# Maxima on ScalarE's queue, normalisation a stage ahead with a second image buffer, staggered last steps

## The chip, the cores and the metric

The kernel runs on one core of one Trainium2 chip. The metric is the device time of one execution in microseconds, the median over the runs shown. All numbers here come from one profiled execution and three timed ones of the kernel before the change.

## What is computed

Sixteen images of 256 channels and 28 x 28 pixels go through a group normalisation, two "codebook" 3 x 3 convolutions with batch normalisation, a squeeze-and-excite gate and two residual additions, all in float32:

```python
def amm_conv3x3(x, centroids, w_sub, stride=1):        # C = 256 channels, k = 16 codes, s = 9 taps
    patches = conv_general_dilated_patches(x, (3, 3), (stride, stride), 'SAME')
    p = patches.reshape(B, C, s, Ho * Wo).transpose(0, 3, 1, 2)
    d = sum(p * p)[..., None] - 2.0 * einsum('bncs,cks->bnck', p, centroids) + sum(centroids * centroids)
    attn = softmax(-d, axis=-1)
    lut = einsum('cks,cso->cko', centroids, w_sub)
    return einsum('bnck,cko->bno', attn, lut)          # reshaped to B, 256, 28, 28

g = _gn(x)                                             # 32 groups
out = relu(bn(amm_conv3x3(g, centroids1, wsub1)))
out = bn(amm_conv3x3(out, centroids2, wsub2))
out = se_layer(out)                                    # mean, two small matmuls, sigmoid gate
return x + relu(out + g)
```

## The kernel before

One *stage* is one convolution of one image. The stages run in the order (0,0), (0,1), (1,0), (0,2), (1,1), (0,3), ...: the first convolution of image b+1 stands between the two convolutions of image b, so that the patches of one stage are prepared while another computes. After the first two stages and up to the last two, stages of the second and of the first convolution alternate; one of each is called a *period* here, and there are fourteen of them before the last pair.

A stage has 16 *units*: two pixel ranges (`PXT`: 384 and 400 of the 784 pixels) by eight groups of 32 channels. A unit runs through these steps:

- `patches`: SP (SyncE's queue) issues four loads of some 110 KB, the unit's rows, from the DRAM buffer `pat` into one of four `pt` tiles.
- `b_logits`, line 543: 16 small matmuls on PE; `b_exp`, line 601: two exponentials on ACT; `b_num`, line 611: 16 small matmuls; `b_turn`, lines 623 and 629: two transposes and a reciprocal on DVE; `c_scale`, line 639: products on POOL; `c_turn`, line 657: a transpose on DVE; `c_look`, line 675: the large 128 x 128 matmuls ("look-ups") that accumulate the output. A look-up is one matmul of the program and two in the trace.
- Four of the 16 units of a second-convolution stage are *maxed* (`MAXED`): their softmax needs a maximum first. Such a unit has its patches in a `pm` tile, and runs ahead: `a_logits` and `a_turn`, `a_max`, `m_turn` (line 575, the tile `mt`), then `m_out` (line 582) sends the maxima to DRAM (`dm`) and `m_in` (line 588) loads them back, spread, into rows of the `pm` tile, which `b_logits` then reads.

The order is written out by hand. `Plan` puts each step into a numbered slot, one slot for each unit, and into a position within the slot: `LOGITS, EXP, LOOK_A, NUM, TURN, SMALL, LOOK_B, MAX, LOOK_C, TURN_BACK, REST`. `emit` walks through slots and positions and issues the steps; every engine and every queue then works through its own instructions in that order. Within a unit's slot s the patches are issued at s - 3 (`lead`), and a maxed unit's first part starts at s - 5 (`lb`). Look-ups are spread over the slots, four or five in each, and two more in a slot that has a `MAX` step.

Around the units, each stage needs:

- `norm`: `load_x` (POOL's queue) brings an image into `xt` (784 KB), `gn_stats` on DVE, `gn_mean` and `gn_var` (small matmuls, small POOL operations), `gn_apply` on ACT writes the padded image `im0`.
- `prep`: `shift` (ACT copies `im` into two shifted `side` images) and twelve `to_pat` steps (line 454), each a 588 KB write from ACT's queue into a `pat` buffer in DRAM. There are three `pat` buffers, and in most of the run each convolution has one.
- `close`, after a second-convolution stage: `se_hidden`, `se_gate`, `se_scale`, then for four pieces of the image `gate` (ACT), and `finish`, which is a DVE operation (line 511), a ReLU on ACT (line 512) and an addition on POOL (line 513), and `store` on POOL's queue. `load_x` is called a second time for this residual. `xpool` has one buffer.

SP's and ACT's transfers share eight completion semaphores, which the program hands out in turn: a transfer is issued only when the one that had its semaphore before it, the eighth before it in the planned order, has landed, whichever of the two queues that one is on.

Within a period the slots are numbered 0 to 15 for the second-convolution stage and 16 to 31 for the first-convolution stage. The places before: `prep` of the next second convolution in slots 16 to 21 (two `to_pat` a slot), the residual's `load_x` in slot 16, `close` in 19 to 24, `norm`'s `load_x` in 25 and its steps in 28 to 32, `prep` of the next first convolution in slots 1 to 12 (one a slot).

Of the kernel before, what the change touches and what calls it, by code (L numbers as in the profile page):

```python
# [8 lines left out]
F32 = mybir.dt.float32  # L9
# [6 lines left out]
P = 128  # L16
H = W = 28
HW = H * W
# [51 lines left out]
def kernel(  # L70
# [71 lines left out]
    xpool = ctx.enter_context(tc.tile_pool(name="xpool", bufs=1))  # L142
# [97 lines left out]
    def scratch(n):  # L240
        return epool.tile([P, 2, 400], F32, tag="e", name="scratch").rearrange("p i m -> p (i m)")[:, :n]

    def sort_channels():
# [19 lines left out]
        row = scratch(C)  # L263
# [124 lines left out]
    epool = ctx.enter_context(tc.tile_pool(name="epool", bufs=4))  # L388
# [118 lines left out]
    def finish(b, k, i):  # L507

        y, xt = ys[b][0][half(k, i)], xs[b][half(k, i)]
        rstd, _ = nrm[b]  # L510
        nc.vector.scalar_tensor_tensor(y, xt, rstd[:, k : k + 1], y, op0=ALU.mult, op1=ALU.add)  # L511
        nc.scalar.activation(y, y, AF.Relu)  # L512
        nc.gpsimd.tensor_add(y, y, xt)
# [64 lines left out]
    def m_out(u):  # L578

        d = drot.tile([4 * 256, 32], F32, tag="dm", name="dm")  # L580
        for p0, n in ((0, P), (P, 96)):
            nc.sync.dma_start(view(d, 32 * p0, [[32, n], [256 * 32, 4], [1, 32]]), u["mt"][:n])
# [125 lines left out]
    class Plan:  # L708
# [12 lines left out]
        def emit(self):  # L721
            for n0, of in self.tiles:

                slots = [n0 + (LC + q) * self.step for q in range(NQ)]
                more = [2 if (s, MAX) in self.jobs else 0 for s in slots]
                k, room = 0, len(LOOKS) - sum(more)
                for q, s in enumerate(slots):
                    n = (q + 1) * room // NQ - q * room // NQ + more[q]
                    for i, (m, o, h) in enumerate(LOOKS[k : k + n]):
                        self.at(s, LOOK_A if i < 2 else LOOK_B if i < n - more[q] else LOOK_C, c_look, of[m], o, h)  # L730
                    k += n
            for key in sorted(self.jobs):
                for f, a in self.jobs[key]:
                    f(*a)

        def stage(self, l, b, pat, s0, maxed):
            at = self.at
            for pi, px in enumerate(PXT):
                n0 = s0 + pi * NQ * self.step
                of = []  # L740
                for m in range(NQ):
# [3 lines left out]
                    if m in maxed:  # L745
                        a = s - self.lb
                        at(a - self.lead, REST, patches, u)
# [5 lines left out]
                        at(a + 2, TURN_BACK, m_out, u)  # L753
                        at(a + 3, EXP, m_in, u)
# [25 lines left out]
        def close(self, b, ob, te):  # L780
# [36 lines left out]
    plan = Plan(1, 3, 5)  # L817
    for si, (l, b) in enumerate(stages):
        t = si * NS
        plan.stage(l, b, pat_of(l, b), t, () if l == 0 else MAXED)  # L820
        if l == 0 and b >= 1:
            t0 = t - NS - (1 if b == 1 else 4)
            plan.at(t0 - 3, REST, load_x, b, x[b])
            plan.norm(b, t0)
            plan.prep(0, pat_of(0, b), t0 + 5, 2 if b == 1 else 1)
        if l == 1:
# [3 lines left out]
            plan.close(b, out[b], t + NS + LC)  # L830
# [5 lines left out]
    for j in range(NCH):  # L836
        for s in range(9):
            plan.at(6 + s // 2, REST, place_wd2, j, s)
        for i in range(4):
            for t in range(4):  # L840
                plan.at(12 + i, REST, place_cw2, i, t, j)
            for t in range(2):
                plan.at(16 + i, REST, place_ws2, i, t, j)
            plan.at(20 + i, REST, place_tail, i, j)
    plan.at(16, REST, setup_codes, 1)
# [15 lines left out]
    with tc.If(flag > 0):  # L861
        with tc.For_i(0, B) as bi:
            load_x("g", x[bass.ds(bi, 1)].rearrange("o c n -> (o c) n"))
            plan = Plan(8, 2, 5)
            plan.norm("g", 0)
            plan.prep(0, d_pat[0], 5, 1)
            s0 = 28
            plan.stage(0, "g", d_pat[0], s0, range(NQ))
            plan.prep(1, d_pat[1], s0 + plan.end, 1)
            s1 = s0 + plan.end + 24  # L870
            plan.stage(1, "g", d_pat[1], s1, range(NQ))
            plan.at(s1 + plan.end - 4, REST, load_x, "g", x[bass.ds(bi, 1)].rearrange("o c n -> (o c) n"))
            plan.close("g", out[bass.ds(bi, 1)].rearrange("o c n -> (o c) n"), s1 + plan.end)
# [75 lines left out]
```

## Time and profile before

| what | value |
|---|---|
| median of 3 runs | 3377.37 us (3372.45 to 3379.37) |
| the profiled execution | 3372.49 us, span 3371.0 us |
| PE busy | 3042.2 us, 90% of the span |
| DVE, POOL, ACT busy | 2250.0, 1501.8, 1094.9 us |
| mean granted TensorE clock | 0.950 |
| DMA moved | 530.24 MB, 157 GB/s in the mean |

PE is the engine to read first: its idle time, and the stretches in which its clock is below one, are what stands above the work itself. Waits are listed with what ended them. Queues are named by the engine that issues on them, with a q (SPq, ACTq).

### The profile page before, as it was taken

Reading aid. Unit: us, or ns where it says so; the run is one execution under the profiler, and the core shown is the slowest. Engines: PE = TensorE matmul, PEld = TensorE weight load, DVE = VectorE, ACT = ScalarE, POOL = GpSimd, SP = SyncE. Lnnn points to the kernel's source line nnn. Section 1 sums busy time; section 2 is a strip of 40 time slices with the busy share of each in tenths; the row PEclk is TensorE's granted clock in tenths of the full one; section 3 lists DMA queues with packets and bytes.
Section 4 is the critical chain, followed back from the end, with each engine's and each line's share of the span. In section 5 each row is a group of like instructions: output and inputs, shape, how many; then the busy total and the mean of one; then the engine's idle time right before and its main releaser. Section 6 shows DMA issues by size and latency. Waiting matters only on the chain.

```text
span 3371.0 us, 94072 instructions
## 1 busy us (share of the span) xinstructions
PE 3042.2 (90%) x39838; PEld 1195.0 (35%) x39838; DVE 2250.0 (67%) x2756; ACT 1094.9 (32%) x1611; POOL 1501.8 (45%) x2165
## 2 busy tenths in 40 slices
PE   4878989999899999999999899999999899999997
PEld 2333333333333333333333333333333333333333
DVE  2355668676675767767676676767767576776785
ACT  2322333333333333333333333333333333333233
POOL 1333454454444445454454445445444444545444
PEclk9888999999999999999999999999999999999998
DMA  6755665746567565665746566475665747566542
GB/s 196 200 117 128 161 194 133 189 121 165 168 149 192 126 177 143 166 194 123 195 123 163 168 166 195 121 181 134 168 183 141 197 124 182 145 156 190 147 100 66
DMA packets 331902, 530.24 MB, mean 157 GB/s; under 512 B 93664, under 2 KB 251088, under 8 KB 331472
## 3 DMA queue, kind: packets, MB, share of 16 engines
q1 hardware_dynamic: 242512, 251.70, 29.8%
q10 hardware_dynamic: 82048, 233.89, 26.7%
q0 software_dynamic: 6912, 38.54, 3.4%
q8 instruction: 316, 5.18, 0.6%
q14 instruction: 114, 0.93, 0.1%
HBM read 269.96 MB, written 254.05 MB: 155 GB/s over the span
## 4 chain that ended last, share of the span: by engine, by line
PE 62%; DMA 16%; DVE 12%; issue 4%; ACT 2%; POOL 2%; SPq 1%; ACTq 1%; DVEq 0%; POOLq 0%
PE acc L675 35%; PE pair L611 13%; PE pair L543 12%; DMA pt<-pat 6%; DVE nt L623 4%; DMA pm<-dm 3%; DMA dm<-mt 3%; DMA pat<-side 2%; DVE q L657 2%; DMA pat<-im 2%; DVE y L511 2%; DVE rc L629 1%; DVE mx L567 1%; ACT e L601 1%; POOL k L639 1%
## 5 line engine op out<-in xcount | busy, mean ns | idle before, releaser
L675 PE MATMUL acc<-q,ws 128*128 128x384 f32 (+1 forms) x4096 | 1701.7, 537 | 0.0
L623 DVE STREAM_TRANSPOSE nt<-pair 128x832 f32<-128x832 f32 (+1 forms) x1024 | 978.3, 993 | 1042.8 <-PE pair L611 907.8
L639 POOL TENSOR_TENSOR k<-nt,rc 128x832 f32<-128x832 f32 (+1 forms) x512 | 803.5, 1569 | 1829.7 <-DVE rc L629 1827.4
L601 ACT ACTIVATE e<-pair 128x800 f32<-128x800 f32 (+1 forms) x1024 | 787.0, 820 | 1692.4 <-PE pair L543 1691.9
L675 PEld LDWEIGHTS acc<-q,ws 128*128 128x128 f32 x4096 | 721.8, 196 | 957.6 <-issue 641.2
L611 PE MATMUL pair<-e,cw 32*32 32x384 f32 (+1 forms) x16384 | 624.0, 527 | 83.6 <-ACT e L601 83.6
L543 PE MATMUL pair<-pt,wd 19*32 19x384 f32 (+1 forms) x14336 | 479.0, 513 | 76.2 <-DMA pt<-pat 75.7
L657 DVE STREAM_TRANSPOSE q<-k 128x832 f32<-128x832 f32 (+1 forms) x512 | 488.9, 955 | 0.8 <-POOL k L639 0.8
L629 DVE RECIPROCAL rc<-nt 128x104 f32<-128x104 f32 (+1 forms) x512 | 398.4, 778 | 17.6
L611 PEld LDWEIGHTS pair<-e,cw 32*32 32x32 f32 x16384 | 179.6, 106 | 452.5 <-ACT e L601 384.3
L543 PEld LDWEIGHTS pair<-pt,wd 19*32 19x32 f32 x14336 | 113.8, 104 | 364.3 <-issue 221.4
L645 POOL TENSOR_TENSOR tail<-nt,rc 128x104 f32<-128x104 f32 (+1 forms) x512 | 236.0, 461 | 0.0
L675 PE MATMUL acc<-qt,ws 128*128 128x400 f32 (+1 forms) x512 | 220.9, 514 | 0.0
L651 POOL TENSOR_TENSOR total<-total,nt 128x96 f32<-128x96 f32 (+1 forms) x448 | 208.9, 466 | 0.0
L543 PE MATMUL pair<-pm,wd 19*32 19x384 f32 (+3 forms) x4096 | 131.1, 541 | 77.4 <-DMA pm<-dm 71.0
L651 POOL TENSOR_TENSOR total<-total,rc 128x96 f32<-128x96 f32 (+1 forms) x448 | 177.2, 396 | 0.0
L562 DVE STREAM_TRANSPOSE z<-pair 128x768 f32<-128x768 f32 (+1 forms) x128 | 121.2, 985 | 12.8 <-PE pair L543 12.4
L675 PEld LDWEIGHTS acc<-qt,ws 128*128 128x128 f32 x512 | 93.4, 192 | 96.0 <-issue 43.9
L567 DVE TENSOR_REDUCE mx<-z 128x48 f32<-128x768 f32 (+1 forms) x128 | 120.8, 944 | 0.0
L512 ACT ACTIVATE y<-y 128x392 f32<-128x392 f32 x64 | 33.9, 529 | 176.4 <-DVE y L511 176.2
L543 PEld LDWEIGHTS pair<-pm,wd 19*32 19x32 f32 (+1 forms) x4096 | 31.1, 105 | 150.4 <-DMA pm<-dm 56.5
L664 DVE STREAM_TRANSPOSE qt<-tail 128x416 f32<-128x416 f32 (+1 forms) x128 | 69.9, 546 | 0.0
(105 smaller groups left out, 726.2 us busy)
## 6 DMA issues: line engine op xcount, KB each, us to landing
pat<-side ACTq DMA_DIRECT2D x256, 588.0 KB
pt<-pat SPq DMA_DIRECT2D x896, 112.5 KB
pt<-pat SPq DMA_DIRECT2D x896, 108.0 KB
pat<-im ACTq DMA_DIRECT2D x128, 588.0 KB
xt<-in_x POOLq DMA_DIRECT2D x32, 784.0 KB, 7.8
pm<-pat SPq DMA_DIRECT2D x128, 112.5 KB
pm<-pat SPq DMA_DIRECT2D x128, 108.0 KB
out_dram<-y POOLq DMA_DIRECT2D x16, 784.0 KB, 5.4
```

The costliest lines, as they stand in the source:

```text
L543: nc.tensor.matmul(ps[t // 2][c : c + 32, t % 2, :n], lhsT=wd[l][32 * i : 32 * i + rows, 4 * u["m"] + t, :], rhs=u["pt"][32 * i : 32 * i + ...
L562: nc.vector.transpose(z[:, : 64 * nb].rearrange("p (t m) -> p t m", t=2), ps[:, :, : 32 * nb])
L567: nc.vector.tensor_reduce(u["mx"][:, 2 * v : 2 * v + 2].rearrange("p t (j b) -> p t b j", j=2)[:, :, :nb], u["z"].pop(0)[:, : 64 * nb].rea ...
L601: nc.scalar.activation(e[:, :, :n], ps[:, :, :n], AF.Exp, scale=2.0)
L611: nc.tensor.matmul(u["nm"][t // 2][32 * i : 32 * i + 32, t % 2, :n], lhsT=cw[l][c : c + 32, 4 * u["m"] + t, :], rhs=es[t // 2][c : c + 32, ...
L623: nc.vector.transpose(nt[:, :nb, 2 * v : 2 * v + 2].rearrange("p b t r -> p t b r"), ps[:, :, : 32 * nb].rearrange("p t (b r) -> p t b r", ...
L629: nc.vector.reciprocal(rc[:, : 8 * nb], u["nt"][:, :, SUM])
L639: nc.gpsimd.tensor_tensor(q[:, :nb].rearrange("p b (a s) -> p (b a) s", s=8), nt[:, :, :8], rc.unsqueeze(2).to_broadcast([P, 8 * nb, 8]), ...
L645: nc.gpsimd.tensor_tensor(tails[key][:, :nb, 8 * (m % 4) : 8 * (m % 4) + 8], nt[:, :, 8].rearrange("p (b a) -> p b a", a=8), rc.rearrange( ...
L651: nc.gpsimd.tensor_add(t[:, : 8 * nb], t[:, : 8 * nb], v)
L657: nc.vector.transpose(q[:, :, : 32 * nb].rearrange("p h (b r) -> p h b r", r=32), u.pop("k")[:, :nb].rearrange("p b (h r) -> p h b r", h=2),)
L675: nc.tensor.matmul(accs[key][:, :n], lhsT=ws[l][:, 2 * m + h if h < 2 else 2 * NQ + m // 4, o * P : (o + 1) * P], rhs=u["q"][h][:, :n], st ...
```

## The change

1. `m_out` and `m_in` move from SP's queue to ACT's; the first part of a maxed unit starts six slots ahead and no longer five, its patches stay in the same slot; `m_out` goes from the end of slot s - 3 to its `TURN` position, `m_in` from `EXP` to `TURN` of slot s - 2.
2. `norm` and `prep` of the first convolution move a stage ahead. `xpool` gets two buffers (`epool` goes from four to two to make room, and the setup's scratch tiles move to other pools), `load_x` moves to slot 16, the same slot as the residual's, the statistics to 19 and 21, mean and variance to 23 and 24, `gn_apply` to 25 and 26, the twelve `to_pat` to slots 28 to 39, that is 28 to 31 and 0 to 7 of the next period. There are four `pat` buffers, two for each convolution.
3. `finish` is split into `finish`, `relu` and `residual`, one slot apart, with one piece of the image a slot (two a slot for the last two images); `store` moves from slot 24 to 27.
4. The look-ups between logits and numerators are half of a slot's, where they were always two: three in a slot of five.
5. The setup's 74 moves of rearranged weights go out four a slot in slots 6 to 24; they had been bunched by kind, up to eight a slot. `setup_codes(1)` moves from slot 16 to slot 20, the second image's `norm` two slots ahead.

```diff
-    d_pat = [dram.tile([NRT * ROWS, HW], F32, name=f"pat{i}") for i in range(3)]
+    d_pat = [dram.tile([NRT * ROWS, HW], F32, name=f"pat{i}") for i in range(4)]
-    xpool = ctx.enter_context(tc.tile_pool(name="xpool", bufs=1))
+    xpool = ctx.enter_context(tc.tile_pool(name="xpool", bufs=2))
-    epool = ctx.enter_context(tc.tile_pool(name="epool", bufs=4))
+    epool = ctx.enter_context(tc.tile_pool(name="epool", bufs=2))
...
         nc.vector.scalar_tensor_tensor(y, xt, rstd[:, k : k + 1], y, op0=ALU.mult, op1=ALU.add)
+
+    def relu(b, k, i):
+        y = ys[b][0][half(k, i)]
         nc.scalar.activation(y, y, AF.Relu)
-        nc.gpsimd.tensor_add(y, y, xt)
+
+    def residual(b, k, i):
+        y = ys[b][0][half(k, i)]
+        nc.gpsimd.tensor_add(y, y, xs[b][half(k, i)])
...
-            nc.sync.dma_start(view(d, 32 * p0, [[32, n], [256 * 32, 4], [1, 32]]), u["mt"][:n])
+            nc.scalar.dma_start(view(d, 32 * p0, [[32, n], [256 * 32, 4], [1, 32]]), u["mt"][:n])
-            nc.sync.dma_start(
+            nc.scalar.dma_start(
                 u["pt"][MROW + j :: 32, :, :n],
...
-                        self.at(s, LOOK_A if i < 2 else LOOK_B if i < n - more[q] else LOOK_C, c_look, of[m], o, h)
+                        self.at(s, LOOK_A if i < n // 2 + n % 2 - more[q] // 2 else LOOK_B if i < n - more[q] else LOOK_C, c_look, of[m], o, h)
...
                         a = s - self.lb
-                        at(a - self.lead, REST, patches, u)
+                        at(a - self.lead + 1, REST, patches, u)
...
                         at(a + 2, TURN_BACK, m_turn, u)
-                        at(a + 2, TURN_BACK, m_out, u)
-                        at(a + 3, EXP, m_in, u)
+                        at(a + 3, TURN, m_out, u)
+                        at(a + 4, TURN, m_in, u)
...
             self.at(t, REST, gn_stats, b, 0)
-            self.at(t + 1, REST, gn_stats, b, 1)
-            self.at(t + 2, SMALL, gn_mean, b)
-            self.at(t + 3, SMALL, gn_var, b)
-            self.at(t + 4, REST, gn_apply, b, 0)
-            self.at(t + 4, REST, gn_apply, b, 1)
+            self.at(t + 2, REST, gn_stats, b, 1)
+            self.at(t + 4, SMALL, gn_mean, b)
+            self.at(t + 5, SMALL, gn_var, b)
+            self.at(t + 6, REST, gn_apply, b, 0)
+            self.at(t + 7, REST, gn_apply, b, 1)
...
-            for k in range(NB):
-                for i in range(2):
-                    self.at(te + 2 + k, REST, gate, b, k, i)
-                    self.at(te + 3 + k, REST, finish, b, k, i)
-            self.at(te + 5, REST, store, b, ob)
+            for n, (k, i) in enumerate((k, i) for k in range(NB) for i in range(2)):
+                self.at(te + 2 + n // 2, REST, gate, b, k, i)
+                self.at(te + 3 + n // pace, REST, finish, b, k, i)
+                self.at(te + 4 + n // pace, REST, relu, b, k, i)
+                self.at(te + 5 + n // pace, REST, residual, b, k, i)
+            self.at(te + 5 + 3 // pace, REST, store, b, ob)
...
-        if l == 0:
-            return d_pat[2 if b == 1 else 0]
-        return d_pat[0 if b == B - 1 else 1]
+        return d_pat[2 * l + b % 2]
...
-    plan = Plan(1, 3, 5)
+    plan = Plan(1, 3, 6)
...
-        if l == 0 and b >= 1:
-            t0 = t - NS - (1 if b == 1 else 4)
-            plan.at(t0 - 3, REST, load_x, b, x[b])
-            plan.norm(b, t0)
-            plan.prep(0, pat_of(0, b), t0 + 5, 2 if b == 1 else 1)
+        if l == 0 and b == 1:
+            plan.at(-4, REST, load_x, b, x[b])
+            plan.norm(b, -3)
+            plan.prep(0, pat_of(0, b), 5, 2)
+        elif l == 0 and b > 1:
+
+            t0 = t - 2 * NS
+            plan.at(t0, REST, load_x, b, x[b])
+            plan.norm(b, t0 + 3)
+            plan.prep(0, pat_of(0, b), t0 + 12, 1)
...
-            plan.close(b, out[b], t + NS + LC)
+            plan.close(b, out[b], t + NS + LC, 1 if b < B - 2 else 2)
...
+    for i, (f, *a) in enumerate(moves):
+        plan.at(6 + i // 4, REST, f, *a)
+    plan.at(20, REST, setup_codes, 1)
```

The same edits reach the loop at the kernel's end, which runs only when a check on the sums fails.

More of the change, by code (lines that the diff above doesn't have):

```diff
@@ L863 @@
             load_x("g", x[bass.ds(bi, 1)].rearrange("o c n -> (o c) n"))
-            plan = Plan(8, 2, 5)
+            plan = Plan(8, 3, 6)
             plan.norm("g", 0)
-            plan.prep(0, d_pat[0], 5, 1)
-            s0 = 28
+            plan.prep(0, d_pat[0], 8, 1)
+            s0 = 32
             plan.stage(0, "g", d_pat[0], s0, range(NQ))
-            plan.prep(1, d_pat[1], s0 + plan.end, 1)
+            plan.prep(1, d_pat[2], s0 + plan.end, 1)
             s1 = s0 + plan.end + 24
-            plan.stage(1, "g", d_pat[1], s1, range(NQ))
+            plan.stage(1, "g", d_pat[2], s1, range(NQ))
             plan.at(s1 + plan.end - 4, REST, load_x, "g", x[bass.ds(bi, 1)].rearrange("o c n -> (o c) n"))
-            plan.close("g", out[bass.ds(bi, 1)].rearrange("o c n -> (o c) n"), s1 + plan.end)
+            plan.close("g", out[bass.ds(bi, 1)].rearrange("o c n -> (o c) n"), s1 + plan.end, 1)
             plan.emit()
```

20 lines of the change are left out of this document (7 added, 13 removed).

## Prediction

> **What bounds the kernel now.** I read the page first, then the waits by engine, then PE's instructions in order of time over one period.
>
> ```profile
> span 3371.0 us, 94072 instructions
> PE 3042.2 (90%) x39838; PEld 1195.0 (35%) x39838; DVE 2250.0 (67%) x2756; ACT 1094.9 (32%) x1611; POOL 1501.8 (45%) x2165
> ...
> PE acc L675 35%; PE pair L611 13%; PE pair L543 12%; DMA pt<-pat 6%; DVE nt L623 4%; DMA pm<-dm 3%; DMA dm<-mt 3%; DMA pat<-side 2%; DVE q L657 2%; DMA pat<-im 2%; DVE y L511 2%; DVE rc L629 1%; DVE mx L567 1%; ACT e L601 1%; POOL k L639 1%
> ```
>
> PE is the bound: 90% busy, and three matmul lines carry 60% of the chain that ended last. What can be won is the other 329 us and the time in which PE's clock is low. PE's waits over the whole run, then one of ACT's and one of SP's queue (total, times, longest):
>
> ```profile
> PE pair L611 <- ACT e L601: 83.6, 49, 4.0
> PE pair L543 <- DMA pt<-pat: 81.9, 32, 11.7
> PE pair L543 <- DMA pm<-dm: 71.0, 24, 4.5
> PE pair L409 <- DVE gn_mv L404: 35.8, 15, 12.2
> ```
> ```profile
> ACT y L512 <- DVE y L511: 176.2, 60, 7.9
> ```
> ```profile
> SPq L582 <- DVE mt L575: 381.4, 54, 19.9
> ```
>
> Four causes hold 272 us of PE's idle time. To see what each costs with its after-effects I take PE's rows of one period (start, length, instruction, idle before) and measure a slot from one start of line 611 to the next.
>
> ```profile
> 1448.91 1.09 PE L611 MATMUL pair<-e,cw 32*32 32x384 f32 x32
> ...
> 1456.71 1.57 PE L543 MATMUL pair<-pt,wd 19*32 19x384 f32 x26 [3.19 <-DMA pt<-pat]
> ...
> 1461.07 1.58 PE L611 MATMUL pair<-e,cw 32*32 32x384 f32 x32
> ...
> 1477.67 1.08 PE L611 MATMUL pair<-e,cw 32*32 32x384 f32 x32
> ...
> 1486.60 2.23 PE L611 MATMUL pair<-e,cw 32*32 32x384 f32 x32 [3.37 <-ACT e L601]
> ...
> 1495.01 1.63 PE L611 MATMUL pair<-e,cw 32*32 32x400 f32 x32 [1.81 <-ACT e L601]
> ...
> 1529.91 0.95 PE L611 MATMUL pair<-e,cw 32*32 32x400 f32 x32
> 1532.55 0.39 PE L409 MATMUL pair<-gn_mv,gmat 128*128 128x4 f32 x2 [1.68 <-DVE gn_mv L404]
> ...
> 1538.90 1.64 PE L611 MATMUL pair<-e,cw 32*32 32x400 f32 x32
> ...
> 1575.17 1.14 PE L611 MATMUL pair<-e,cw 32*32 32x384 f32 x32
> ...
> 1577.73 0.93 PE L543 MATMUL pair<-pt,wd 19*32 19x384 f32 x32
> ...
> 1579.34 0.81 PE L675 MATMUL acc<-q,ws 128*128 128x384 f32 x2
> 1580.08 1.14 PE L611 MATMUL pair<-e,cw 32*32 32x384 f32 x32
> ...
> 1584.98 1.14 PE L611 MATMUL pair<-e,cw 32*32 32x384 f32 x32
> ...
> 1591.84 1.41 PE L543 MATMUL pair<-pm,wd 21*32 21x400 f32 x32 [1.86 <-DMA pm<-dm]
> ...
> 1595.87 0.95 PE L611 MATMUL pair<-e,cw 32*32 32x400 f32 x32
> ...
> 1605.62 1.22 PE L611 MATMUL pair<-e,cw 32*32 32x400 f32 x32
> ...
> 1610.68 1.17 PE L611 MATMUL pair<-e,cw 32*32 32x400 f32 x32
> ...
> 1616.60 1.65 PE L543 MATMUL pair<-pm,wd 21*32 21x400 f32 x32 [3.21 <-DMA pt<-pat]
> ...
> 1621.14 1.64 PE L611 MATMUL pair<-e,cw 32*32 32x400 f32 x32
> ```
>
> An undisturbed slot with four look-ups is 1575.17 to 1580.08, 4.9 us; a fifth look-up adds 0.8 (the row of two), and a slot with a maxed unit's first logits adds two look-ups and 0.9, which makes 7.4. Against that:
>
> - Slot 18, a `pt` load late: 12.2 less 5.7 (five look-ups) is 6.5 over, of which 3.2 are idle.
> - Slots 22 and 23, exponentials late (`close`): 8.9 less 5.7 and 8.4 less 4.9 make 6.7 over, 5.2 idle.
> - Slot 30, `gn_mean` waits for the statistics: 9.0 less 4.9 is 4.1 over, 1.7 idle.
> - Slots 7 and 11, maxed logits late: 10.9 less 7.4 and 10.5 less 4.9 make 9.1 over, 5.1 idle. The label `pt<-pat` at 1616.60 is the row of a `pm` matmul that needs `m_in`; the chain below shows the same two transfers behind it.
>
> Over is more than idle because PE runs slowly after a stop: 32 matmuls of line 543 take 0.93 undisturbed, 26 take 1.57 behind the stop at 1456.71; line 611 goes from 1.1 to 1.6. The clock of that stretch says the same (length, PE, clock, DMA share, GB/s):
>
> ```profile
> 1457.00:1470.00 13.00, 13.00 (x151) 0.79 0.75 229
> ```
>
> The Trainium skill, "TensorE: Matmul & The Clock Gate", section "What's actually happening", has the clock halved only after an idle window of about 3.4 us. The trace does not agree: after 1.68 us idle at 1532.55 the next line 611 row takes 1.64, as slow as after 3.21. By that rule short stops would cost only themselves, and the change could win no more than the idle of three causes, 190 us, which is 3182 before what it adds; the row speaks against it, and it gets no chance of its own.
>
> **The change part by part.**
>
> *Maxima on ACT's queue.* Why they are late, from the chain (start, length): slots 6 to 10 of this period, then the longest in and out of others.
>
> ```profile
> 1579.02 4.93 DMA pat<-side
> 1583.97 4.90 DMA dm<-mt
> ...
> 1589.51 2.19 DMA pm<-dm
> ...
> 1606.52 0.32 DVE mt L575
> ```
> ```profile
> 2006.23 6.52 DMA pm<-dm
> ...
> 3190.28 7.51 DMA dm<-mt
> ```
>
> `m_turn` of slot 9 ends at 1606.8, 1.2 us after slot 10's line 611 began (1605.62): DVE finishes a slot's list only in the next. From there out, in and the issue of both take until 1616. SP stands in this wait (381 us in the row above), and the `pt` loads stand behind it. After the change `m_turn` is in slot s - 4, one slot of 4.9 us earlier. ACT comes to `m_out` right after its exponentials, waits some 1.2 us for `mt`, issues, and meets `m_in` about 4 us later. Out takes 4.90 in the chain's row, so `m_in` goes out after at most 1 us more of waiting, and lands 2.2 to 6.5 later; it has 7 us until the maxed logits. ACT has 7 us from `m_out` to the exponentials that come behind `m_in`. Behind the waiting ACT also stand the `to_pat` write of that slot, which now has six slots of reserve, and through the shared semaphores SP's loads eight transfers later, more than a slot behind. So the 9.1 go, but for new small waits: bounds 0 (all hidden) and 3 a period (ACT held at three of the four units by an out like the 7.51, 1 us each); I take 1, since 4.90 is the ordinary row.
>
> By the Trainium skill, "DMA: Bandwidth & Descriptors", section "Queues, rings and completion order", each queue is one ring on the same DMA engines, taken in order. That speaks against this part: `m_out` now stands behind 588 KB writes on ACT's ring, where it had stood behind 110 KB loads. The write before it starts a slot earlier, and 4.93 is what one took; so by the rows it has just landed. By the rule with a full ring it would not have; that is the third rival.
>
> *`finish`, `relu`, `residual` apart.* ACT stood 176 us for line 511, with the next exponentials behind it. With the ReLU a slot later its input is done before ACT arrives (DVE's `finish` is one instruction of about 1.0 a slot):
>
> ```profile
> 1482.12 1.96 DVE L511 SCALAR_TENSOR_TENSOR y<-xt,gn_rstd,y 128x392 f32<-128x392 f32 x2
> ```
>
> The 6.7 go. DVE has the cover: 2250 of 3371 us busy; without it one `finish` a slot would be 1 us late. POOL's additions are off PE's path.
>
> *Normalisation a stage ahead.* The statistics now lie where DVE has no maxed unit's transposes and two slots before `gn_mean`: the stop in slot 30 goes. In other periods it is smaller than here: 35.8 less the start's 12.2, over 14 periods, is 1.7 idle, times 1.7 (all four causes: 26.4 over, 15.2 idle) makes 2.9. `prep` moves from slots 1 to 12 to 28 to 7, with the same twelve writes; it was not late before, so this wins nothing. The maxed units' patches have one slot less until they are read; SP no longer stands in front of them.
>
> *The second image load in slot 16.* This is the cost. Slot 16 starts twelve `to_pat` writes, two a slot, and one image load, and slot 18 waits for `pt`:
>
> ```profile
> 1445.44 11.23 DMA pt<-pat
> ```
> ```profile
> SPq L530 <- DMA pat<-im: 12.9, 2, 11.6
> ```
> ```profile
> DMA to landing us min/median/max: 4.8/7.8/11.8
> ```
>
> SP was first held 11.6 us by a `pat<-im` write through the shared semaphores (window 1425 to 1460; the load reads another buffer), then one 110 KB load took 11.2. An image load takes 4.8 in quiet and up to 11.8 here. The stop in slot 18 stays: nothing in the change loosens that chain. The second image load follows the first on POOL's ring, so the squeeze lasts longer. Bounds: 0, since the DMA share is 0.75 from 1457 on, behind the first load (13 us at 229 GB/s with a quarter unused is room for about 1 MB, and the load is 784 KB); and 9, when the loads starve for another 11.8 us, less the 5 us by which the next unit's load is ahead of its logits (one slot), and PE restarts slowly (2.4 over idle, as in slot 30). I take 4, a little under the middle, since the quarter unused and the 11.2 us are both rows of this very place. The statistics on DVE wait for the second load too; by slot 19 it has had 15 us and more.
>
> *Look-ups, `epool`, four `pat` buffers, setup.* `e` has two buffers for two tiles a unit; PE has read both before the next logits exist: nothing. In undisturbed slots PE does not wait for the exponentials, so the third look-up ahead of the numerators wins nothing. The moves of the setup run through SP beside the first images' writes: half of slots 18 to 22 get two transfers more, and slots 12 to 15 four fewer. No row prices it; between -10 (the size of the row's 12.2 start stop) and +10; I take 0.
>
> **The sum**, from the profiled execution, 3372.5, over 14 periods: maxima 14 x (9.1 - 1) = 113; `close` 14 x 6.7 = 94; norm 14 x 2.9 = 41; second image load 14 x 4 = 56 back. 192 us net, and the last pair's maxed units have the same two waits, 9 more: 3372.5 - 201 = 3171. The median of the runs lies 5 us over the profiled one: 3176; I say 3180.
>
> **The rivals.**
>
> *A. The image loads starve SP.* If the second load costs its upper 9 and the maxima's small waits 3 a period, the sum is 14 x (6.1 + 6.7 + 2.9 - 9) + 9 = 103, and 3275. For it: 11.2 us for one small load. Against it: the share of 0.75 behind.
>
> *B. The image load is hidden.* 14 x (9.1 + 6.7 + 2.9) + 9 = 271, and 3107. For it the quarter unused; against it the stop of slot 18 itself.
>
> *C. ACT held by `m_in`, and slower than before.* If `m_out` lies behind a whole `to_pat` write (4.93) and then takes 4.90, it lands 10 us after its issue where ACT has 7; the next exponentials are 3 late, the maxed logits behind them 2 more. Three of the four units meet a `to_pat`; each then costs 5 idle and 2.4 of slow clock, 22 a period. With 18.7 won, and 22 and the 4 of the image load lost, 14 x 7.3 = 102 slower: 3480. It decides where three times (idle + 2.4) passes 18.7 - 4, at 2.5 idle, an out of about 7.5 us. For it: the row of 7.51, and 4.90 right behind a `pat<-side`. Against it: the write before `m_out` starts a slot earlier and has just landed.
>
> *D. The stops only move.* `close` and the maxima hid late `pt` loads; without them the loads are late themselves, by as much: then only norm's 41 and half of the maxima remain, less 56, about 3330.
>
> **How the numbers follow.** Forecast 0.55, A 0.18, B 0.12, C 0.08, D 0.07. The forecast's own range is 3130 to 3235 (image load 1.5 to 7, with 15 us for the rest). With A and B the range is 3095 to 3285; C and D, 0.15, are left out. A change within 0.2%, 7 us, is what the three runs spread over and can't be told from none. Faster by more: forecast, A, B and 0.04 of D, 0.89. Same 0.02 and slower 0.01 are the rest of D, with the image load at its upper end; with C slower is 0.09.
>
> **What would show it.** In the waits after: PE for `pm<-dm` from 71 to under 15, for exponentials from 83.6 to under 20, ACT line 512's successor for DVE near 0, PE for `gn_mv` near the start's 12; SP no longer waits for `mt`. PE for `pt<-pat` stays over 60 and may grow to over 100, in slots 18 to 21: that is the image load. In A it is over 150. In C ACT's exponentials are held and PE waits for them in slots 29 to 8. Wrong would be: `pm<-dm` still over 40, or a new stop of DVE at the statistics (line 403) for the image.

## The result, and the profile after

The changed kernel takes 3125.25 us in the median of four runs (3097.23 to 3131.95), beside 3378.37 (3372.45 to 3385.60) for the kernel before on the same chip: a ratio of 0.923, interval 0.917 to 0.929. The profiled execution has 3126.19 us with a span of 3124.6, which is 246.4 less than the span before; the sum of the prediction was 201. The 3125 lies 5 us under the forecast's own range (3130 to 3235) and inside the wider one that takes in rivals A and B (3095 to 3285). Lines from 514 on stand six higher in the changed kernel: 601 became 607, 611 became 617, 543 became 549, 675 became 681.

First the span and the engines, from the page:

```profile
span 3124.6 us, 94006 instructions
PE 2951.3 (94%) x39838; PEld 1167.1 (37%) x39838; DVE 2255.7 (72%) x2756; ACT 1094.0 (35%) x1611; POOL 1504.2 (48%) x2165
```

PE does the same 39838 instructions in 91 us less, with a mean granted clock of 0.974 where it was 0.950, and is idle 155 us less. Idle time and slow clock went together. PE's waits over the whole run (total, times, longest):

```profile
PE pair L617 <- ACT e L607: 60.1, 41, 4.5
PE pair L549 <- DMA pt<-pat: 22.5, 3, 11.6
PE pair L409 <- DVE gn_mv L404: 12.1, 1, 12.1
PE pair L420 <- POOL gn_dv L414: 11.7, 14, 0.8
PE pair L549 <- DMA pm<-pat: 10.5, 16, 3.5
```

The row `pm<-dm` (71.0) is gone from the view, `gn_mv` is down to the start's 12.1, and `pt<-pat` fell from 81.9 to 22.5, 11.6 of which is one wait at the start. Only the exponentials' row is still large. ACT's and SP's queues tell why:

```profile
ACT e L607 <- DMA dm<-mt: 118.5, 33, 8.3
ACT y L703 <- PE acc L681: 76.3, 31, 9.9
ACT e L607 <- DMA pt<-pat: 71.1, 12, 7.1
```
```profile
SPq L536 <- PE pair L549: 661.1, 276, 10.7
SPq L536 <- DMA pat<-im: 318.4, 62, 11.0
SPq L536 <- DMA pat<-side: 298.7, 113, 23.6
SPq L536 <- DMA dm<-mt: 283.2, 66, 11.5
```

The first of these rows stood at this before the change:

```profile
SPq L530 <- PE pair L543: 335.6, 215, 10.6
```

SP no longer waits for `mt`. What ends its waits most is now PE's logits, which free the `pt` buffers, 661 us where it was 336: SP more often stands at the end of its four buffers. It still stands behind ACT's transfers through the shared semaphores, behind the maxima's way out too (283 us), but PE seldom feels it (22.5 us). ACT waits instead, for the maxima's way out (`dm<-mt`, mostly hidden) and, with the next exponentials behind it, for a `pt` load: a patch write on ACT's queue shares its semaphore with one of SP's loads.

Where the time went, slot by slot: the start-to-start times of line 611 (617 after) in both traces, summed over the 14 periods for groups of slots; this accounts for the whole span.

| slots | before | after | difference | the prediction's sum |
|---|---|---|---|---|
| 0 to 17 (maxima) | 1477.8 | 1379.6 | -98.1 | -113 |
| 18 to 21 (`pt` late, image loads) | 386.9 | 385.8 | -1.1 | +56 |
| 22 and 23 (`close`) | 239.4 | 139.8 | -99.6 | -94 |
| 24 to 29 | 491.6 | 489.7 | -1.8 | 0 |
| 30 and 31 (`gn_mean`) | 218.5 | 189.5 | -29.0 | -41 |
| start, first two stages, last two | 556.8 | 540.2 | -16.6 | -9 |

Of the 45 us by which the sum fell short, 57 lie in slots 18 to 21; the other rows miss by 12 or so in all, the other way. So the open question is that row: the stop did not grow, and it is not the same stop. Before, slot 18 held it (12.2 in the period shown). After, this is the same place, slots 18 to 20, as PE's rows and ACT's (start, length, instruction, idle before):

```profile
1338.75 0.93 PE L617 MATMUL pair<-e,cw 32*32 32x384 f32 x32
...
1343.92 1.58 PE L617 MATMUL pair<-e,cw 32*32 32x384 f32 x32 [0.36 <-ACT e L607]
...
1353.05 1.82 PE L617 MATMUL pair<-e,cw 32*32 32x384 f32 x32 [3.43 <-ACT e L607]
1354.80 1.01 PE L482 MATMUL pair<-se_hid,w_sb 16*128 16x1 f32 x4
1355.73 2.93 PE L681 MATMUL acc<-q,ws 128*128 128x384 f32 x4
...
1362.96 0.88 PE L617 MATMUL pair<-e,cw 32*32 32x384 f32 x6
```
```profile
1345.82 0.25 ACT L475 ACTIVATE se_hid<-pair,b_sb 16x1 f32<-16x1 f32 x1 [1.25 <-PE pair L469]
1349.03 3.06 ACTq L454 DMA_DIRECT2D pat<-side  x2
1352.18 1.51 ACT L607 ACTIVATE e<-pair 128x768 f32<-128x768 f32 x2 [6.11 <-DMA pt<-pat]
```

Slot 18 takes 5.2 now. Slot 19 takes 9.1: ACT had nothing to do after 1346.1 and its queue stood at two patch writes, the second of which went out only after a `pt` load (the releaser in the last row) had landed; the exponentials behind it started at 1352.18, and PE, its logits long done, had idled 3.43. Slot 20 takes 9.9 with no idle of note, since the clock is low: a row of four look-up matmuls takes 2.93 where 1.56 is usual. The window of the stop says the same (length, then the busy time of PE, PEld, DVE, ACT and POOL, then clock, DMA share and GB/s):

```profile
1348.00:1362.00 14.00, 10.57 (x95) 4.59 (x80) 5.99 (x11) 3.64 (x7) 4.98 (x8) 0.72 0.89 268
```

The DMA engines are 0.89 busy here, and an image load takes 9.7 us in the median, where it took 7.8:

```profile
xt<-in_x POOLq DMA_DIRECT2D x32, 784.0 KB, 9.7
```

### The profile page after: what moved, and what is told of

The parts are those of the page before. It is cut to its first block, busy times and chain, and to the rows that moved or that the text cites. A ratio compares the mean times of both kernels' runs of the same rounds, so it can differ in the third digit from the quotient of the medians.

```text
span 3124.6 us, 94006 instructions
## 1 busy us (share of the span) xinstructions
PE 2951.3 (94%) x39838; PEld 1167.1 (37%) x39838; DVE 2255.7 (72%) x2756; ACT 1094.0 (35%) x1611; POOL 1504.2 (48%) x2165
## 5 line engine op out<-in xcount | busy, mean ns | idle before, releaser
L681 PE MATMUL acc<-q,ws 128*128 128x384 f32 (+1 forms) x4096 | 1662.4, 525 | 5.3 <-ACT y L703 5.3
L681 PEld LDWEIGHTS acc<-q,ws 128*128 128x128 f32 x4096 | 704.9, 191 | 917.0 <-issue 595.1
L617 PE MATMUL pair<-e,cw 32*32 32x384 f32 (+1 forms) x16384 | 601.3, 509 | 60.5 <-ACT e L607 60.1
L549 PE MATMUL pair<-pt,wd 19*32 19x384 f32 (+1 forms) x14336 | 439.2, 509 | 22.8 <-DMA pt<-pat 22.5
L617 PEld LDWEIGHTS pair<-e,cw 32*32 32x32 f32 x16384 | 169.7, 103 | 414.0 <-ACT e L607 382.8
L651 POOL TENSOR_TENSOR tail<-nt,rc 128x104 f32<-128x104 f32 (+1 forms) x512 | 244.8, 478 | 0.0
L657 POOL TENSOR_TENSOR total<-total,nt 128x96 f32<-128x96 f32 (+1 forms) x448 | 200.2, 447 | 0.0
L549 PE MATMUL pair<-pm,wd 19*32 19x384 f32 (+3 forms) x4096 | 147.4, 502 | 10.7 <-DMA pm<-pat 10.5
L693 ACT ACTIVATE im<-acc,bnsh,bnsc 128x384 f32<-128x384 f32 (+1 forms) x64 | 43.4, 678 | 154.5 <-PE acc L681 154.5
L703 ACT ACTIVATE y<-acc,bnsh,bnsc 128x384 f32<-128x384 f32 (+1 forms) x64 | 43.4, 678 | 91.6 <-PE acc L681 76.3
```

The source lines that it names most:

```text
L549: nc.tensor.matmul(ps[t // 2][c : c + 32, t % 2, :n], lhsT=wd[l][32 * i : 32 * i + rows, 4 * u["m"] + t, :], rhs=u["pt"][32 * i : 32 * i + ...
L617: nc.tensor.matmul(u["nm"][t // 2][32 * i : 32 * i + 32, t % 2, :n], lhsT=cw[l][c : c + 32, 4 * u["m"] + t, :], rhs=es[t // 2][c : c + 32, ...
L651: nc.gpsimd.tensor_tensor(tails[key][:, :nb, 8 * (m % 4) : 8 * (m % 4) + 8], nt[:, :, 8].rearrange("p (b a) -> p b a", a=8), rc.rearrange( ...
L657: nc.gpsimd.tensor_add(t[:, : 8 * nb], t[:, : 8 * nb], v)
L681: nc.tensor.matmul(accs[key][:, :n], lhsT=ws[l][:, 2 * m + h if h < 2 else 2 * NQ + m // 4, o * P : (o + 1) * P], rhs=u["q"][h][:, :n], st ...
```

## The experiments

Each profile was accounted by slots as above; the table gives differences to the kernel before, in us over 14 periods. They are those of one profiled execution of each kernel, which can lie 20 us off the median (e3: 3329.66, the median 3349.90). Slots 13 to 17 and 24 to 29 (-9 to +4) and the ends (-1 to -29) are left out. The ratio is that to the kernel before on the same chip. Lengths of single slots in the text below are medians over the 14 periods, unless a mean is named.

| kernel | median | ratio, interval | 0-5 | 6-12 | 18-21 | 22-23 | 30-31 |
|---|---|---|---|---|---|---|---|
| changed kernel | 3125.25 | 0.923 (0.917 to 0.929) | +13 | -116 | -1 | -100 | -29 |
| e1: `close` alone | 3280.41 | 0.967 (0.964 to 0.971) | 0 | +6 | +7 | -92 | +6 |
| e2: maxima alone | 3258.01 | 0.961 (0.958 to 0.965) | +26 | -94 | +2 | -4 | -34 |
| e3: norm alone | 3349.90 | 0.990 (0.987 to 0.993) | 0 | -69 | +30 | +2 | -2 |
| e7: changed, maxima on SP | 3200.07 | 0.946 (0.943 to 0.949) | +4 | -89 | +13 | -97 | +12 |
| e8: changed, setup as before | 3140.69 | 0.927 (0.924 to 0.930) | +15 | -115 | +5 | -101 | -30 |
| e4: changed, both loads early | 3076.00 | 0.908 (0.905 to 0.911) | +13 | -103 | -70 | -93 | -31 |
| e9: changed, norm's load early | 3090.07 | 0.915 (0.911 to 0.919) | +16 | -115 | -38 | -95 | -30 |
| e5: changed, writes spread | 3134.39 | 0.926 (0.923 to 0.929) | +16 | -98 | -94 | -102 | +56 |
| e6: e4 and e5 | 3144.05 | 0.929 (0.926 to 0.932) | +14 | -93 | -94 | -102 | +54 |
| e10: before, load early | 3393.15 | 1.002 (1.000 to 1.005) | +1 | +32 | -15 | +1 | +1 |
| e12: e7, both loads early | 3233.25 | 0.955 (0.951 to 0.960) | +1 | -34 | -7 | -101 | +17 |
| e11: changed, loads in 11 and 13 | 3058.38 | 0.903 (0.899 to 0.907) | +15 | -115 | -72 | -96 | -31 |

**The three parts alone** (e1, e2, e3), each put into the kernel before. e1, with two pieces of the image a slot where the change has one:

```diff
+    def relu(b, k, i):
+        y = ys[b][0][half(k, i)]
         nc.scalar.activation(y, y, AF.Relu)
...
-                    self.at(te + 3 + k, REST, finish, b, k, i)
...
+                self.at(te + 3 + n // 2, REST, finish, b, k, i)
+                self.at(te + 4 + n // 2, REST, relu, b, k, i)
+                self.at(te + 5 + n // 2, REST, residual, b, k, i)
```

> The kernel before, with only the last steps of an image taken apart (finish, ReLU and residual each a slot later than the one before, two of them a slot). Theory 1 (the terms add up): slots 22 and 23 lose their 6.7 us in each of 14 periods, 94 us less, 3284; PE's wait for the exponentials falls from 83.6 to under 40 and ACT's wait for DVE line 511 from 176 to near 0; slots 7, 11, 18 and 30 keep their stops. Rival (the stops only move): the time that slots 22 and 23 give up comes back as later pt loads or other stops of PE, and the kernel is less than 45 us faster, over 3333.

Measured 0.967, 3280. The term holds and stands where it was put: -92 in slots 22 and 23, and `pt` loads and other stops took back only some 8 of it in all. PE's waits for the exponentials fell to 15.7 (the lines of e1 stand six higher too):

```profile
PE pair L549 <- DMA pm<-dm: 78.3, 28, 3.8
PE pair L549 <- DMA pt<-pat: 78.3, 31, 11.5
PE pair L409 <- DVE gn_mv L404: 35.6, 15, 12.0
PE pair L617 <- ACT e L607: 15.7, 20, 2.4
```

e2 moves the maxima only:

```diff
-            nc.sync.dma_start(view(d, 32 * p0, [[32, n], [256 * 32, 4], [1, 32]]), u["mt"][:n])
+            nc.scalar.dma_start(view(d, 32 * p0, [[32, n], [256 * 32, 4], [1, 32]]), u["mt"][:n])
...
-            nc.sync.dma_start(
+            nc.scalar.dma_start(
                 u["pt"][MROW + j :: 32, :, :n],
...
-                        at(a + 2, TURN_BACK, m_out, u)
-                        at(a + 3, EXP, m_in, u)
+                        at(a + 3, TURN, m_out, u)
+                        at(a + 4, TURN, m_in, u)
...
-    plan = Plan(1, 3, 5)
+    plan = Plan(1, 3, 6)
```

> The kernel before, with only the maxima moved: their writes and reads on ACT's queue, and the maxed unit's first steps one slot earlier. Theory 1 (terms add up): slots 7 and 11 lose 8.1 to 9.1 us a period, 113 to 127 us less, 3251 to 3265; slot 18 keeps its late pt load, since one image load and twelve writes still start in slot 16. Rival 1: SP, no longer standing in the wait for mt, runs further ahead, and the late pt load of slot 18 goes too, which adds up to 14 x 6.5 = 91 more: 3165 to 3180; PE's wait for pt loads then falls from 81.9 to under 35. Rival 2 (ACT held by its own transfers): 3378 or slower, with PE waiting for the exponentials in slots 29 to 8.

Measured 0.961, 106 less by the profiled spans. The maxima's term holds in its size. Slot 18's late `pt` load goes, as the first rival has it, but nothing is won by that: slot 18 falls from 11.2 to 5.8, slots 19 and 20 take 8.5 and 8.7, and slots 18 to 21 together the same as before. The stop changes its kind: PE's wait for the exponentials rises from 83.6 to 159.9, and ACT's queue shows patch writes that wait for one another, with the exponentials behind them.

```profile
PE pair L611 <- ACT e L601: 159.9, 88, 5.0
PE pair L543 <- DMA pt<-pat: 34.5, 8, 11.9
```
```profile
ACT e L601 <- DMA dm<-mt: 106.8, 31, 3.5
ACT e L601 <- DMA pat<-side: 92.3, 16, 8.9
```

There is only one image load in slot 16 here. So the stop that the changed kernel has in slots 19 and 20 does not need the second load; it comes with the maxima on ACT's queue (e7, below, changes the queue alone, and the stop is back in slot 18).

e3 moves the normalisation and the first convolution's patch writes only:

```diff
-    xpool = ctx.enter_context(tc.tile_pool(name="xpool", bufs=1))
+    xpool = ctx.enter_context(tc.tile_pool(name="xpool", bufs=2))
...
-            t0 = t - NS - (1 if b == 1 else 4)
-            plan.at(t0 - 3, REST, load_x, b, x[b])
...
+            t0 = t - 2 * NS
+            plan.at(t0, REST, load_x, b, x[b])
+            plan.norm(b, t0 + 3)
+            plan.prep(0, pat_of(0, b), t0 + 12, 1)
```

> The kernel before, with only the normalisation and the patch writes of the first convolution a stage ahead (second image buffer, both image loads in slot 16, four patch buffers, two exponentials' buffers). Theory 1 (the prediction's terms): 41 us won in slot 30, 56 lost behind the second image load in slots 18 to 21, 15 slower, 3393. Rival 1: the second load is hidden and only the 41 is left, 3337. Rival 2: the load costs here what the stop in slots 19 and 20 of the changed kernel costs (6.8 us a period over the undisturbed length) on top of slot 18's 6.5, so 95 less 41, some 54 slower, 3432.

Measured 0.990, 34 faster by the ratio: near the first rival's number, but not for its reason. The load is not hidden: slots 18 to 21 are 30 longer, 2.2 a period. And the 41 of slot 30 do not come. The stop there is gone (`gn_mv` is back to 12.2 in all), but slot 31, which the maxed logits share, takes 10.4 in the mean where it took 8.2:

```profile
1510.61 1.17 PE L611 MATMUL pair<-e,cw 32*32 32x400 f32 x32
...
1517.72 0.94 PE L543 MATMUL pair<-pm,wd 21*32 21x384 f32 x32 [2.01 <-DMA pm<-dm]
```

What was won lies in slots 6 to 12, 69 us: slot 11 falls from 10.1 to 5.1. The patch writes had stood in slots 1 to 12, beside the maxima's transfers of slots 10 and 11; now they end in slot 7. Of the steps that e3 moves, they alone stood in slots 8 to 12. So slot 11's stop had two causes, and either part alone takes it away: e2 won 94 in these slots and e3 69, the change 116.

**Queue or slot?** e7 puts `m_out` and `m_in` of the changed kernel back on SP's queue (`nc.scalar` to `nc.sync` in both) and keeps the earlier slot.

> The changed kernel, with the writes and reads of the maxima put back on SP's queue; the slot that they were moved forward stays. Theory 1 (the earlier slot does it: DVE has the transposed maxima ready before the queue comes to the write): 3125 to 3150, and PE's wait for pm<-dm stays near 0. Rival (the queue does it: SP stands in front of the write again, and the pt loads behind it are late): SP waits for mt again for over 200 us in all, slots 7 and 11 or the stops for pt<-pat return, and the time is 3180 to 3260. A third way: ACT, freed of its waits for dm<-mt (118 us), gives back the 1.0 us each of slots 2 and 30, 3095 to 3110.

Measured 3200, the rival's range: the queue is worth 2.3 points of the ratio, about 75 us. Slot 18 is back at 12.4, now in place of 19 and 20, and PE waits for `pt` loads as before the change:

```profile
PE pair L549 <- DMA pt<-pat: 77.3, 28, 12.0
PE pair L549 <- DMA pm<-pat: 32.1, 33, 1.7
PE pair L617 <- ACT e L607: 16.3, 23, 3.5
```

SP waits less for `mt` than the rival had it (over 200), since the earlier slot has it ready more often, but stands as long for its way out:

```profile
SPq L594 <- DMA dm<-mt: 132.1, 82, 4.5
SPq L588 <- DVE mt L581: 97.4, 20, 13.9
```

The third way did not show: slot 2 gets 0.7 back, but slot 6 is 1.9 longer and slot 30 2.8.

**The setup.** e8 is the changed kernel with the setup's moves bunched as before.

> The changed kernel, with the transfers of the setup put back where they were before (up to eight in one slot, in slots 6 to 23 of the first stages). The prediction took 0 for this part, between 10 less and 10 more. If the spreading is what made the second stage 129.6 us long in place of 139.3, this is 10 slower, 3135, and the second stage 139; if it is nothing, 3125 and 130. The periods after it are the same in both.

The second stage is 139.5 us long in e8 and 129.6 in the changed kernel, as expected of the spreading. The whole time, 0.927 against 0.923, has intervals that overlap: the runs do not tell these two apart.

**What makes the stop of slots 18 to 20?** In e4 both image loads leave slot 16, in e5 the second convolution's patch writes go one a slot from slot 9, in e6 both.

```diff
# e4
-            plan.at(t0, REST, load_x, b, x[b])
+            plan.at(t0 - 8, REST, load_x, b, x[b])
...
-            plan.at(t + NS, REST, load_x, b, x[b])
+            plan.at(t + NS - 12, REST, load_x, b, x[b])
# e5
-            plan.prep(1, pat_of(1, b), t - NS + (LC if near else 0), 3 if near else 2)
+            plan.prep(1, pat_of(1, b), t - NS + (LC if near else -7), 3 if near else 1)
```

> The changed kernel, with both image loads taken out of slot 16: the one for the residual in slot 4, the one for the normalisation in slot 8. In the changed kernel slots 19 and 20 take 8.6 and 8.9 us where 5.1 and 5.4 are the undisturbed lengths, since ACT stands at the patch writes of slots 17 and 18 with the next exponentials behind them. Theory L (the image loads fill the DMA engines, the transfers that ACT waits for land late): slots 19 and 20 fall to under 5.7, 14 x 6.8 = 95 faster, about 3030, and ACT's waits for pat and pt before the exponentials (71 us for pt<-pat) go. Theory P (two patch writes a slot on ACT's queue are enough, and the image loads only sit beside them): slots 19 and 20 stay above 7.5, within 30 of 3125. For theory P: with the maxima alone moved, where only one image load starts in slot 16, slots 19 and 20 take 8.4 and 8.7 all the same.

> The changed kernel, with the second convolution's twelve patch writes started one a slot in slots 9 to 20 in place of two a slot in 16 to 21 (the first and the last image as they were); the image loads stay in slot 16. Theory P: slots 19 and 20 fall to under 5.7, 14 x 6.8 = 95 faster, about 3030. Theory L: they stay above 7.5, within 30 of 3125. A third way: the writes now meet those of the maxima in slots 10 and 11, and these slots become longer by what 19 and 20 lose.

> The changed kernel, with both edits: image loads in slots 4 and 8, the twelve patch writes one a slot in 9 to 20. If one of the two carries the stop of slots 19 and 20, this is as fast as that one alone (3030, within 15); if each is half of it, 95 here and 40 to 60 with each alone; if the writes spread over slots 9 to 20 meet the load of slot 8, slots 8 to 12 grow and it is slower than the better one alone.

e4 takes 3076: slots 19 and 20 fall to 5.6 and 5.8, which is theory L's sign, with some 50 us where 95 were expected; slots 10, 11, 21 and 22 take some of it back. e5 empties the same slots too (5.2 and 5.4), so theory P's sign as well: loads and writes make the stop only together. But e5 is no faster than the changed kernel. What slots 18 to 21 lose, 93, slots 30 and 31 gain, 85: slot 30 takes 14.2. Its maxed unit's loads go out later on SP, behind a patch write that had the semaphore before (PE's rows, then SP's wait from 1395 to 1415):

```profile
1409.32 1.63 PE L617 MATMUL pair<-e,cw 32*32 32x400 f32 x32 [0.34 <-ACT e L607]
...
1414.02 0.83 PE L549 MATMUL pair<-pm,wd 19*32 19x384 f32 x2 [1.53 <-DMA pm<-pat]
1415.23 0.83 PE L549 MATMUL pair<-pm,wd 19*32 19x384 f32 x2 [0.38 <-DMA pm<-pat]
1416.40 2.06 PE L549 MATMUL pair<-pm,wd 19*32 19x384 f32 x28 [0.35 <-DMA pm<-pat]
```
```profile
SPq L536 <- DMA pat<-im: 17.4, 1, 17.4
```

e6 is as e5: with the writes spread, nothing is left for the loads to win.

**The price of the second load, and the load without the rest.** e9 makes only the first edit of e4. e10 is the kernel before with the residual's load in slot 4 (second edit of e4, two image buffers, two exponentials' buffers). e12 is e7 with both edits of e4.

> The changed kernel, with only the normalisation's image load taken from slot 16 to slot 8; the residual's stays in 16. It prices the second load of slot 16. The prediction's term: 4 us a period, 56 faster, 3069, as fast as with both loads early (3076). Against it, with the maxima alone moved and one load in slot 16, slots 19 and 20 were 8.4 and 8.7 long, so one load is enough for the stop: 3110 to 3125, and slots 19 and 20 above 7.5.

> The kernel before, with the residual's image load in slot 4 in place of 16 (two image buffers, two buffers for the exponentials, to make room for it). The prediction held that slot 18's late pt load (6.5 us over) comes from the image load beside the writes of slot 16. If so, slot 18 falls from 11.2 to under 6, PE's wait for pt<-pat from 81.9 to under 35, and it is 14 x 5.5 = 77 faster or more, 3300. If it comes from SP's place behind a patch write (the shared semaphores) alone, slot 18 stays above 9, within 30 of the kernel before. The load may cost something where it goes, since slots 7 and 11 wait for the maxima's transfers there.

> The changed kernel, with the maxima's transfers on SP's queue and the image loads in slots 8 and 4. With them on SP and the loads in slot 16 it took 3200, with slot 18 at 12.4. If the loads make that stop too, slot 18 falls to under 6, 14 x 7 = 98 faster, 3100, and ACT's queue is worth only the 25 to 30 of slots 6 and 30. If SP's standing in front of the maxima makes it, slot 18 stays above 9, 3170 or more.

e9: 3090, so one load of the two is worth 0.9 points, some 29 us, of which slots 18 to 21 show 37, 2.6 a period: between the two expectations. The intervals of e9 and the changed kernel touch, so the slots carry this more than the times. Slot 19 keeps 7.1.

e10: slot 18 falls to 5.8, so the image load did make that late `pt` load. Nothing comes of it: slot 21 goes from 4.9 to 8.7, where the next late load stands (1.84 idle), and slot 6, where the load now is, from 4.9 to 6.4.

```profile
1471.54 0.84 PE L543 MATMUL pair<-pt,wd 19*32 19x384 f32 x6
1474.22 0.92 PE L543 MATMUL pair<-pt,wd 19*32 19x384 f32 x26 [1.84 <-DMA pt<-pat]
```

e12 gives the same with the rest of the change in place: 18 falls to 5.2, 21 rises to 11.0, slot 6 to 12.8, and it is slower than e7. With the maxima on SP's queue a freed stop comes back some slots later. With them on ACT's, e4 keeps what it frees. With the loads early the queue is worth 157 us (3233 against 3076), with the loads in slot 16 only 75.

**A better place for the loads.** e11 is the changed kernel with the loads in slots 11 and 13 (`t + NS - 5` and `t0 - 3` in the lines of e4), where neither patch writes nor maxima start.

> The changed kernel, with the loads in slots 13 (normalisation) and 11 (residual), where no patch write and no transfer of the maxima starts. With loads in slots 8 and 4, slots 10, 11, 21 and 22 were together 1.8 us longer in the mean than in the changed kernel. If those 1.8 come from the load in slot 8 beside the maxima, this is up to 14 x 1.8 = 25 faster than 3076, 3050. If a load in 13 still fills the queues when the writes of slot 16 begin, slots 19 and 20 grow again, above 6.5, and it is slower than 3076.

Measured 3058, 0.903: faster than the changed kernel by two points and than the kernel before by 9.7%. The intervals do not tell it from e4 (0.908); the slots do: 6 to 12 are 12 us shorter. Slots 10 and 11 are back at their undisturbed length (4.8, 5.7), 19 and 20 at 5.6 and 5.7. An image load takes 5.2 us in the median, and the stretch that was the stop runs at full clock with the DMA engines as busy as there (the load; the window; one of PE's rows in it):

```profile
xt<-in_x POOLq DMA_DIRECT2D x32, 784.0 KB, 5.2
```
```profile
1320.00:1337.00 17.00, 16.89 (x260) 6.63 (x228) 12.38 (x18) 6.58 (x13) 8.32 (x14) 1.00 0.89 254
```
```profile
1324.37 1.57 PE L617 MATMUL pair<-e,cw 32*32 32x384 f32 x32
```

## Why the prediction came out as it did

- **What bounds the kernel: right.** PE's stops and the slow clock behind them were what could be won, and all of the 246 us lie there, 155 in PE's idle time and 91 in its busy time, where the same instructions run at a higher mean clock. Two of the signs that were named did not come: the wait for `pt` loads was to stay over 60 (22.5), that for exponentials to fall under 20 (60.1).
- **Maxima: right in size, for a cause too few.** The sum had 113, 8.1 a period; slots 0 to 17 gave 98 in the change, 7.0 a period. Rival C's mechanism is there (ACT waits 118.5 us for `dm<-mt`), but in the change most of those waits end before PE is due. Alone (e2) some show: slots 0 and 1 are 1.8 longer there. What the step didn't see is that slot 11's stop also hung on the patch writes beside it.
- **`close`: right.** 6.7 a period predicted, 7.1 measured in the change and 6.6 alone.
- **Norm: near in amount by luck, wrong in place.** "The stop in slot 30 goes" is true, but alone it is worth 2 us in slots 30 and 31, as slot 31's maxima then wait. The 29 that the change has there come with the maxima's move (-34 alone). Moving `prep` was costed at nothing, "it was not late before, so this wins nothing"; it freed slot 11, 69 us in slots 6 to 12 of e3.
- **The second image load: the step that failed.** Two sentences of it. The cost, 4 a period or 56, measured 2.2 (e3) and 2.6 (e9), 30 to 37: the term was mis-sized by a third to a half, to the upper side. And "the stop in slot 18 stays: nothing in the change loosens that chain" is wrong: the maxima's move off SP's queue does (e2: slot 18 at 5.8; e7: back at 12.4). It didn't win the 6.5 either, because ACT's patch writes then hold the exponentials at the same place, so that the balance of slots 18 to 21 is zero by two effects that the sum had not separated.
- **Rival B**, the image load hidden, gave 3107, nearer to 3125 than the forecast's own 3180, and is not what happened: the load has a price, and taking it away wins 29; that slots 18 to 21 come out at nothing is the balance of the two effects above. **Rival D**, that the stops only move, is false for `close` and the maxima, and true for the stop of slots 18 to 20: in e10, e12 and e5 it moves and costs about as much or more.
- **The ends:** 9 predicted, 17 measured; 10 of them are the second stage, with the setup's moves spread (e8's trace).

Open: the parts alone win 233 us of the 246 by their profiled spans, but this is two errors that cancel. In slots 6 to 12 they add up to -156 and the change has -116, since e2 and e3 win the same stop; in slots 18 to 21 they add up to +39 (7, 2 and 30), and the change has -1. Which of them gives back the 40 beside the others was not separated. Part 4, the look-ups, was run only with the rest. That SP's and ACT's transfers wait for each other through shared semaphores is read from the traces' releasers; no run changed the number of semaphores.

## What to carry to other kernels

Account the traces by place, slot by slot, before crediting a part: one place alone was off by 57 us here, errors of other places had the other sign, and two parts claimed the same stop. Two parts that take away the same stop are worth less than their sum (94 and 69 alone, 116 together), and a stop that hangs on a shared queue moves on when its first cause is taken away, as long as that queue stays behind. Large loads belong where no other transfer that somebody waits for starts: two loads moved by five and three slots won two points more.

## What the runs showed of the hardware beyond that

- A short stop need not slow PE. The prediction read, from 1.68 us of idle with a slow clock behind it, that short stops bring the slow clock. In e10 a stop of 1.84 us (1474.22, above) is followed by 26 matmuls in 0.92, full speed, and the windows show it; before the change, behind the 1.68:

```profile
1474.00:1479.00 5.00, 4.78 (x67) 2.15 (x68) 1.39 (x2) 1.51 (x2) 1.40 (x4) 1.00 0.88 252
```
```profile
1532.60:1539.00 6.40, 6.40 (x58) 2.40 (x70) 3.45 (x4) 1.73 (x3) 3.15 (x6) 0.62 0.39 90
```

  So idle time of one length is followed by both clocks. The Trainium skill, "TensorE: Matmul & The Clock Gate", section "What's actually happening", says that the activity window runs free, so that the moment of a change depends on where in it the work falls; the two rows do not speak against that, though its length of about 3.4 us of idle doesn't explain the slow one. The price of a short stop is then a mean: the four stops of the prediction cost 1.7 times their idle time.

  The clock records of the kernel before bear this out. They hold only 1.0 and 0.5, and 64 of the 65 slow stretches last 3.41 us or two or three times that. Taking PE's stops between 400 and 3000 us that stand alone (full clock in the 3 us before, no other stop over 1 us within 4 us), a slow stretch begins in the stop or within 4.5 us of its end after 7 of the 20 stops of 1.5 to 2.0 us, after 8 of the 14 of 2.0 to 2.5, and after all 27 of 2.5 to 3.4.
- A long row is not yet a slow clock. The prediction also read 1.6 for a row of line 611 as one. In e11 such a row takes 1.57 (1324.37, above) inside a stretch whose clock is 1.00, so it is the windows that show the clock, not these rows.
- Moving a wait off one queue can make the other the one that stands. With the maxima gone from SP, the longest of its waits is for PE's buffers (661 us), and PE's wait for `pt` loads is 22.5 us where it was 81.9; at the same place it is now ACT that waits for a shared semaphore, with the exponentials behind it (71.1 us for `pt<-pat`).
- The same 784 KB load takes 5.2 us in the median in slots 11 and 13 (e11), 9.7 in slot 16 beside the patch writes, and 11.7 in slot 16 of e3, where the maxima are on SP's queue.
